# The last block's row sums, the first accumulation and the first scores of the second head pair, moved in a fused attention kernel

## The chip, the cores and the metric

The kernel runs on one core of a Trainium2 chip. The metric is the device time of one execution in microseconds (us); a version's time is the median of its runs. TensorE does matrix products (PE in the profile, its weight loads PEld), VectorE (DVE) and GpSimd (POOL) elementwise work, ScalarE (ACT) functions, copies and scalings, and SyncE (SP) issues most transfers. Each engine works through its own list of instructions in order; semaphores make one wait for another.

## What is computed

Two layers, one after the other, on x of 4 batches x 64 x 64 x 256 (float32):

```python
# layer 0: self-attention over the 4096 positions of a batch
f = xt @ Wf + bf; g = xt @ Wg + bg; v = xt @ Wh + bh
beta = softmax(einsum('bqd,bkd->bqk', g, f), axis=-1)
x = x + (einsum('bqk,bkd->bqd', beta, v) @ Wo + bo)
# layer 1: triangular attention, 8 heads of 32, then a perceptron
q, k, v1, v2 = (x @ W).reshape(B, N, N, 8, 32)  # for Wq, Wk, Wv1, Wv2
att = softmax(einsum('bilhd,bljhd->biljh', q, k) / sqrt(32), axis=2)
out = einsum('biljh,bilhd,bljhd->bijhd', att, v1, v2)
h = layer_norm(x + out @ Wo)
out = layer_norm(relu(h @ W1 + b1) @ W2 + b2 + h)
```

## The kernel before

The batches are worked through one after the other; what is left of a batch (output projection, norms and perceptron of layer 1) is spread over layer 1 of the next batch. The order of every instruction is written out by hand; there is no scheduler behind it.

**Layer 0** takes the 4096 query positions in 8 blocks of 512. For each block, 32 tiles of scores s (128 keys x 512 queries, line 534) go through an exponential on ScalarE (e, line 546) into the value product o on TensorE (line 561). VectorE adds the exponentials up in esum, four tiles side by side (line 568). At the end of a block, line 571 folds four partial sums into two, and lines 573 to 575 make of these two a pair of tiles: `part[0]` is the sum rounded to float32r (a format that TensorE takes in one pass), `part[1]` the remainder; between them line 574 writes the full sum into esum as well. In `norm`, line 582, two matmuls with a matrix of ones add both over the partitions into den; VectorE takes the reciprocal (line 584) and multiplies o by it (line 586). The projection y follows (lines 607, 608), and then q, k, v1, v2 of layer 1. Seven of the eight blocks do this behind the next block's scores. The last one has no next block: its chain esum, den, reciprocal, oT, y stands at the exit of the layer. There the matmuls hp ("heads", lines 1043 and 1048, the output projection of layer 1 of the batch before) and the rest of the projections of block 6 are put between. The full sum and den also go into a table of bounds (line 594). At the very end of the kernel that table decides whether everything is run once more in a safe form; it isn't, for these data.

**Layer 1** takes the 8 heads in 4 pairs of 2, and each pair in 8 steps: 32 steps. A step's weights come from S (exponentials of the scores sp, lines 872 and 882) through sums, es and a transposition att (line 926). Eight products of the step, m = 0 to 7, multiply att by v2 (line 974): m of 5 and more, in an even step of batches 1 to 3, on GpSimd (Rp), the others on VectorE (R). TensorE adds each up with v1 in two PSUM tiles acc (line 984; a pair of m for each n = m // 2), which ScalarE copies out as ao (line 994). The tile att is copied for GpSimd by ScalarE (attP, line 934), because GpSimd reads it there.

In batches 1 to 3 the order of all this is the list `ORDER` (line 43), walked once per period of two steps in `next_layer1` (line 1508). A word names a piece of work, and the number behind the slash how many periods late it is: `R05/1` is product m = 5 of step 0 of the period before, `A05/1` its accumulation, `T01/1` the copy ao of acc tile 1. `sp` (scores), `e0` and `e1` (their exponentials) stand at one place for all periods but the first; in the first, `sf`, `f0` and `f1` take their place later on. `h1` and `h0` are the two halves of the heads of the tile of 256 tokens two ahead, and the transfer of the next A tile is issued when both halves are made; `ht` the transposition htp of h; `hU` and `hT` its norms on ScalarE (line 1148); `m0` the first half of the perceptron (mp, line 1176), `z0` and `z1` the second (zp, line 1196). `so`, `rr`, `pp`, `fo`, `fa` are the statistics, roots, polish (GpSimd, lines 1104 to 1115) and scalings (ScalarE, line 1120) of the norms: `fo` writes z from zp, `fa` writes h from hp. All words that are not in reach of the first periods do nothing there. So the first period in which accumulations run has, on TensorE, the order A05, A04, z0, z1, t1, A03, A06, A02, A00, A07, A01, t0, sf, h1, h0, ht, A13, A12, A17.

Buffers that matter: PSUM tiles are taken from three pools of two buffers each: `psA` (1024 wide: s, sp, acc and the last block's den), `psB` (512 wide: hp, zp, mp, htp, projections), `psC` (o, att). The SBUF tile `part` shares its buffer with the perceptron's hid and the input tile xin. A transfer takes one of eight semaphores in turn, and is issued only when that semaphore's last transfer has landed; SP and ScalarE each issue from their own list.

## Time and profile before

| | us |
|---|---|
| median of 3 runs | 3689.03 |
| lowest, highest | 3687.88, 3690.12 |
| the profiled execution | 3685.46 |
| its span, from the first to the last instruction | 3683.3 |

The profiled execution is a run of its own; 2.16 us of its time lie outside the span. The mean granted clock of TensorE over the span is 0.994 of full speed. The exits of layer 0 lie at these times: the reciprocal of the last block starts at 411.40 in batch 0, 1276.33 in batch 1, some 2157.3 in batch 2 (its second den matmul starts at 2156.78) and 3038.36 in batch 3. The first scores of the second head pair, sp, start in batches 1 to 3 at 1330.46, 2211.47 and 3092.47.

Times within the span count from its start. A line of the timeline merges neighbouring instructions of one kind: start, time from the first's start to the last's end, engine, line, operation, output<-inputs, shapes, number; in brackets the idle time of the engine before it and what ended it. An fp32 matmul shows as two instructions, its two passes.

### The profile page before, as it was taken

How to read it: one execution, taken by the hardware profiler on the slowest of the kernel's cores; microseconds unless marked ns; L12 is line 12 of the kernel's file. 1: busy time of each engine (PE TensorE's matmuls, PEld its weight loads, DVE VectorE, ACT ScalarE, POOL GpSimd, SP SyncE). 2: the span in 40 equal slices, each digit the busy share in tenths (PEclk: the TensorE clock that was granted, in tenths of full speed). 3: DMA queues.
4: the chain of work that ended last, by engine and by line, in shares of the span. 5: the costliest groups of instructions: out<-in, count | busy, mean ns of one | idle time of the engine just before them, and what ended most of it. 6: DMA issues, size and time to landing. Idle time of an engine off the chain costs nothing.

```text
span 3683.3 us, 58564 instructions
## 1 busy us (share of the span) xinstructions
PE 3562.0 (97%) x22602; PEld 1930.0 (52%) x22602; DVE 2682.3 (73%) x2142; ACT 1963.3 (53%) x4257; POOL 1763.0 (48%) x918
## 2 busy tenths in 40 slices
PE   9999999988999999999999999999899999999998
PEld 6555444444555555554455555554355555555477
DVE  4555599896555569999555449999755456999976
ACT  3444456554444367665444447676544436677654
POOL 5000199895000079999100019999700005999920
PEclk9999999999999999999999999999999999999999
DMA  9111566566111344425311154333511125431221
GB/s 150 47 46 46 145 160 165 147 160 161 49 52 52 94 117 95 93 50 103 70 54 52 49 142 92 75 91 65 118 43 49 52 74 137 97 91 49 68 65 56
DMA packets 461872, 324.01 MB, mean 88 GB/s; under 512 B 300112, under 2 KB 418640, under 8 KB 452752
## 3 DMA queue, kind: packets, MB, share of 16 engines
q1 hardware_dynamic: 412544, 293.21, 29.9%
q0 software_dynamic: 36160, 19.94, 4.6%
q10 hardware_dynamic: 12880, 7.01, 0.7%
q8 instruction: 181, 2.97, 0.4%
q14 instruction: 107, 0.88, 0.1%
HBM read 176.37 MB, written 143.65 MB: 87 GB/s over the span
## 4 chain that ended last, share of the span: by engine, by line
PE 70%; POOL 7%; issue 3%; DMA 3%; DVE 3%; ACT 2%; SPq 0%; ACTq 0%; POOLq 0%; DVEq 0%
PE acc L984 18%; PE o L561 18%; POOL Rp L974 6%; PE proj L622 6%; PE zp L1196 5%; PE mp L1176 5%; PE s L534 5%; PE hp L1043 3%; PE sp L872 3%; PE v1p L654 2%; DVE R L974 1%; PE y L607 1%; PE att L926 1%; PE hp L1048 1%; PE htp L1143 1%
## 5 line engine op out<-in xcount | busy, mean ns | idle before, releaser
L974 POOL TENSOR_TENSOR Rp<-attP,v 128x2048 f32<-128x2048 f32 x328 | 1491.8, 4576 | 420.0 <-ACT attP L934 370.2
L974 DVE TENSOR_TENSOR R<-att,v 128x2048 f32<-128x2048 f32 x696 | 1548.9, 2274 | 91.0 <-PE acc L984 72.5
L561 PE MATMUL o<-e,v 128*128 128x512 f32 x2048 | 1043.4, 592 | 0.0
L568 DVE TENSOR_TENSOR esum<-esum,e 128x2048 f32<-128x2048 f32 x224 | 512.9, 2290 | 551.7 <-ACT e L546 548.8
L546 ACT ACTIVATE e<-s 128x1024 f32<-128x1024 f32 x512 | 524.0, 1025 | 581.5 <-PE s L534 481.9
L534 PE MATMUL s<-gT,fT 128*128 128x512 f32 x1024 | 785.5, 769 | 8.9 <-ACT e L546 5.1
L984 PE MATMUL acc<-R,wsel 128*32 128x512 f32 x5568 | 698.2, 599 | 16.1 <-DVE R L974 8.1
L1104 POOL TENSOR_SCALAR nt<-mv 128x4 f32<-128x4 f32 (+1 forms) x51 | 9.9, 194 | 1202.9 <-DVE mv L1060 1198.8
L561 PEld LDWEIGHTS o<-e,v 128*128 128x128 f32 x2048 | 388.3, 190 | 276.6 <-issue 233.9
L984 PE MATMUL acc<-Rp,wsel 128*32 128x512 f32 x2624 | 346.6, 600 | 27.2 <-POOL Rp L974 26.5
L994 ACT COPY ao<-acc 128x1024 f32<-128x1024 f32 x256 | 254.8, 1021 | 177.3 <-PE acc L984 166.7
L984 PEld LDWEIGHTS acc<-R,wsel 128*32 128x32 f32 x5568 | 154.7, 109 | 354.5 <-issue 277.3
L534 PEld LDWEIGHTS s<-gT,fT 128*128 128x128 f32 x1024 | 193.9, 190 | 244.4 <-issue 231.4
L909 ACT ACTIVATE es<-S,rd 128x64 f32<-128x64 f32 x1024 | 257.8, 336 | 16.2 <-DVE rd L901 13.4
L1176 PE MATMUL mp<-hT,w 128*128 128x256 f32 x1024 | 249.5, 389 | 0.7 <-ACT hT L1148 0.7
L1196 PE MATMUL zp<-w,hid 128*128 128x256 f32 x1024 | 244.9, 384 | 0.8 <-ACT hid L1185 0.8
L1176 PEld LDWEIGHTS mp<-hT,w 128*128 128x128 f32 x1024 | 186.5, 190 | 101.4 <-ACT hid L1185 36.9
L1196 PEld LDWEIGHTS zp<-w,hid 128*128 128x128 f32 x1024 | 185.5, 190 | 62.5 <-issue 31.9
L584 DVE RECIPROCAL rec<-den 128x512 f32<-128x512 f32 x32 | 107.4, 3357 | 133.6 <-PE den L582 133.6
L984 PEld LDWEIGHTS acc<-Rp,wsel 128*32 128x32 f32 x2624 | 80.2, 110 | 209.1 <-issue 124.8
L1185 ACT ACTIVATE hid<-mp,b_sb 128x256 f32<-128x256 f32 x256 | 105.6, 471 | 117.5 <-PE mp L1176 117.5
L882 ACT ACTIVATE S<-sp 128x512 f32<-128x512 f32 x128 | 129.8, 1116 | 62.9 <-PE sp L872 62.9
(179 smaller groups left out, 3595.1 us busy)
## 6 DMA issues: line engine op xcount, KB each, us to landing
v<-v2d SPq DMA_DIRECT2D x44, 512.0 KB
v1c<-v1d SPq DMA_DIRECT2D x128, 128.0 KB
aT<-ao SPq DMA_DIRECT2D x1024, 16.0 KB
A<-aT SPq DMA_DIRECT2D x256, 64.0 KB
out_dram<-z SPq DMA_DIRECT2D x63, 256.0 KB
y<-yT SPq DMA_DIRECT2D x56, 256.0 KB
q<-st SPq DMA_DIRECT2D x56, 256.0 KB
k<-st SPq DMA_DIRECT2D x52, 256.0 KB
```

The source lines that it names most:

```text
L534: nc.tensor.matmul(s_ps[r // 2][:, r % 2, :], fT[tt][:, ts(r * 4 + n, P)], gT[qb // 4][:, ts(qb % 4, QB)], start=True, stop=not safe,)
L546: nc.scalar.activation(e[g][:, 2 * j : 2 * j + 2, :], s_ps[j], AF.Exp)
L561: nc.tensor.matmul(o_ps[qb], F.v[tt][:, r * 4 + n, :], es[:, r, :], start=(k == 0 and r == 0), stop=(k == 7 and r == 3),)
L568: nc.vector.tensor_tensor(esum[qb], esum[qb], es, ALU.add)
L622: nc.tensor.matmul(ps, w[:, cc, rows], y(qb, cc), start=(cc == 0), stop=(cc == 1))
L882: nc.scalar.activation(self.S[pair][:, :, l0 : l0 + 8].rearrange("p i l -> p l i"), sp[:, lh], AF.Copy if self.safe else AF.Exp,)
L909: nc.scalar.mul(e[:, i, :], rows[:, i, :], rec[:, i : i + 1])
L974: eng.tensor_tensor(R, src.unsqueeze(1).to_broadcast([P, D, N]), v2[h], ALU.mult)
L984: nc.tensor.matmul(acc[32 * c : 32 * c + 32, n % 2, :], w[:, n, c, 16 * h : 16 * h + 32], R[:, ts(c, 8), :].rearrange("p d j -> p (d j)"), ...
L994: nc.scalar.copy(self.ao[step][:, ts(np, 2)].rearrange("p k d j -> p k (d j)"), self.acc[step][np])
L1176: nc.tensor.matmul(self.mp[:, fc % 2, :], w1_sb[:, cc, ts(fc, P)], self.hT[tt][:, cc, :], start=(cc == 0), stop=(cc == 1),)
L1196: nc.tensor.matmul(zp[:, n, :], self.hid[tt][:, fc, ts(n, P)], w2_sb[:, fc, :], start=(fc == 0), stop=(fc == 3 and tt not in self.hT2),)
```

## The change

Three edits. The last block of layer 0 (each batch) no longer makes the pair `part`: it writes only the full sum, and one fp32 matmul with the ones read as fp32 takes it to den. In the first period of a batch's layer 1 (batches 1 to 3) the accumulation A05 (of GpSimd's product) is taken out of its place and put behind A04 (of VectorE's product). And `sf`, the first scores of the second pair, moves in `ORDER` from before `R17` and `h1` to behind `h1`; `h0` moves from behind `f0` to before it. In all other periods `sf` and `f0` do nothing, so there the order stays what it was.

```diff
@@ ORDER
-    rr/1 pp/1 W0 R01/1 A07/1 A01/1 fo/1 fa T01/1 R12/1 t0 T00/1 sf/1 R17/1 h1/-1 R13/1 f0/1 h0/-1 ht f1/1 R16/1
+    rr/1 pp/1 W0 R01/1 A07/1 A01/1 fo/1 fa T01/1 R12/1 t0 T00/1 R17/1 h1/-1 sf/1 R13/1 h0/-1 f0/1 ht f1/1 R16/1
@@ values
                 nc.vector.tensor_tensor(halves[:, 0:2], halves[:, 0:2], halves[:, 2:4], ALU.add)
+                if qb == last:
+                    nc.vector.tensor_tensor(halves[:, 2], halves[:, 0], halves[:, 1], ALU.add)
+                    return
                 part = parts_of[qb] = work.tile([P, 2, QB], PART, tag="hid", name="part", bufs=1)
@@ norm
-            two = parts_of.pop(qb)
-            for h in range(2):
-                nc.tensor.matmul(den, ones_f, two[:, h], start=(h == 0), stop=(h == 1))
+            if qb < last:
+                two = parts_of.pop(qb)
+                for h in range(2):
+                    nc.tensor.matmul(den, ones_f, two[:, h], start=(h == 0), stop=(h == 1))
+            else:
+                nc.tensor.matmul(den, ones_f.bitcast(F32), part, start=True, stop=True)
@@ next_layer1
                 i = period - late
-                if word[0] in "RATSWVtc":
+                if i == 0 and word in ("A05", "A04"):
+                    for m in (4, 5) if word == "A04" else ():
+                        step_word("A", 0, m)
+                elif word[0] in "RATSWVtc":
                     step_word(word[0], 2 * i + int(word[1]), int(word[-1]))
```

## The prediction

> **What bounds the kernel now.** I read the page first: the engines' shares, then the chain of waits.

> ```profile
> span 3683.3 us, 58564 instructions
> PE 3562.0 (97%) x22602; PEld 1930.0 (52%) x22602; DVE 2682.3 (73%) x2142; ACT 1963.3 (53%) x4257; POOL 1763.0 (48%) x918
> PE 70%; POOL 7%; issue 3%; DMA 3%; DVE 3%; ACT 2%; SPq 0%; ACTq 0%; POOLq 0%; DVEq 0%
> ```

> TensorE is busy 97% of the span and carries 70% of the chain. So a saving counts only where TensorE stands still, and the edits lie at such places: the exit of the attention layer (four batches) and the first steps of the second layer (batches 1 to 3, counted from 0). I then read the timeline at the exit of batch 1, VectorE first:

> ```profile
> 1272.45 1.23 DVE L571 TENSOR_TENSOR esum<-esum 128x1024 f32<-128x1024 f32 x1
> 1273.71 0.69 DVE L573 TENSOR_TENSOR part<-esum 128x512 fp32r<-128x512 f32 x1
> 1274.32 0.69 DVE L574 TENSOR_TENSOR esum<-esum 128x512 f32<-128x512 f32 x1
> 1275.04 0.69 DVE L575 TENSOR_TENSOR part<-esum,part 128x512 fp32r<-128x512 f32 x1
> 1276.33 3.36 DVE L584 RECIPROCAL rec<-den 128x512 f32<-128x512 f32 x1 [0.59 <-PE den L582]
> ```

> Columns: start, duration, engine, line, instruction, and in brackets the idle time before it and who ended it. TensorE's waits between 1273 and 1340 us:

> ```profile
> PE sp L872 <- ACT ao L994: 1.6, 1, 1.6
> PE acc L984 <- POOL Rp L974: 1.3, 1, 1.3
> PE den L582 <- DVE part L573: 1.2, 1, 1.2
> PE den L582 <- DVE part L575: 0.8, 1, 0.8
> ```

> These four are nearly all its idle time here, and each has an edit. Its timeline around the first two:

> ```profile
> 1316.53 1.07 PE L984 MATMUL acc<-Rp,wsel 128*32 128x512 f32 x8 [1.34 <-POOL Rp L974]
> 1317.41 1.04 PE L984 MATMUL acc<-R,wsel 128*32 128x512 f32 x8
> 1318.38 1.99 PE L1196 MATMUL zp<-w,hid 128*128 128x256 f32 x8
> ...
> 1328.20 0.65 PE L926 MATMUL att<-ident,es 128*128 128x128 f32 x4
> 1330.46 2.08 PE L872 MATMUL sp<-q,k 32*64 32x64 f32 x64 [1.61 <-ACT ao L994]
> 1332.47 1.13 PE L1043 MATMUL hp<-wo,A 128*128 128x256 f32 x4
> 1333.44 0.38 PE L1048 MATMUL hp<-ident,yc 128*128 128x128 f32 x2
> 1333.66 1.03 PE L1043 MATMUL hp<-wo,A 128*128 128x256 f32 x4
> ```

> and what ScalarE does meanwhile:

> ```profile
> 1327.57 1.02 ACT L1120 ACTIVATE z<-zp,rn 128x256 f32<-128x256 f32 x2 [0.62 <-POOL rn L1115]
> 1328.48 1.02 ACT L1120 ACTIVATE h<-hp,rn 128x256 f32<-128x256 f32 x2
> 1329.38 1.94 ACT L994 COPY ao<-acc 128x1024 f32<-128x1024 f32 x2
> ```

> Batch 2 has the same pattern 881.01 us later. Batch 3 differs in one thing; one row per stretch (length, busy time of the engines, TensorE's granted clock, DMA share, GB/s):

> ```profile
> 1328.00:1335.00 7.00, 5.39 (x87) 4.48 (x84) 4.93 (x3) 5.29 (x8) 7.00 (x2) 1.00 0.35 55
> 3090.00:3097.00 7.00, 5.41 (x80) 4.28 (x77) 4.95 (x3) 5.29 (x8) 7.00 (x2) 0.84 0.33 53
> ```

> The clock falls there: sp starts at 3092.47 and the next accumulation at 3098.96, 6.49 us; in batch 1 it is 1330.46 to 1335.27, 4.81 us. The fall costs 1.68 us, and the delay stays: two periods on, the sp at 3135.14 lies 42.67 us behind, in batch 1 (1371.45) 40.99. So time won or lost here is carried on.

> [...] the heads stand 1.61 us behind an sp that waits. [...] here the two y stores hold SP for 6.07 us (1285.60 on).

> **Part 1, the row sums.** Two VectorE additions (L573, L575, 0.69 each) and one of two single-pass matmuls go; one fp32 matmul of two passes comes. The full sum takes L573's place, 1273.71 to 1274.40, so the matmul starts where den starts now, 1274.55. A pair of fp32 passes of this shape takes 1.02 us (o<-e,v x2), so it ends at 1275.57 and the reciprocal starts 0.04 later, 1275.61 instead of 1276.33: 0.72 us. TensorE is free for the heads after 2 x 0.43 us (ten o passes in 4.45), at 1275.41 instead of 1276.13: 0.72 too. What comes next is y, which waits for the product after the reciprocal (0.29 us idle), so both sides move together. Batch 0: 409.63 + 1.02 + 0.04 = 410.69 instead of 411.40, 0.71. Four batches: 2.87 us. The v2 loads, which don't move, are no new bound: the last rows land at 1302.3 in the chain of waits, and the first product starts at 1311.9.

> **Part 2, the accumulations of the first step.** VectorE's product (A04) is done at about 1314.1 (half of its pair from 1311.88), TensorE has finished its heads at about 1315.0, so A04's 0.86 us run inside the 1.34 us of idle time. A05 starts at 1316.53 as now, when GpSimd's first product is there. zp starts at 1317.50 instead of 1318.38: 0.88 us earlier. But GpSimd multiplies without a break from 1311.93 to 1325.52 (three products in 13.59), only then polishes (1325.61), and ScalarE's z, h and ao follow that. ao does not move, so sp does not: the 0.88 us become idle time before the next piece. I count it at 0; both ends of its bound are 0 to 0.1.

> **Part 3, the scores behind the heads.** In the built program the first head's matmuls stand ahead of sp; the other half and htp behind. They need a free PSUM buffer: the semaphore value they wait for is that of z (ends 1328.59), not of h (1329.50). The A tile is no bound: it was issued from 1315.0 on, ahead of the q and k loads in the same queue, whose transfers end at 1330. So the first head runs from about 1328.65, takes 1.08 us (1332.47 to 1333.66 is 1.19 behind sp, the other half 1.08) and ends at 1329.75. sp starts at 1330.46 as before, when ao ends. Behind it only one half is left, so htp starts at 1333.66 instead of 1334.74: 1.08 us. If the buffer came only with h, sp would slip by 0.19 and 0.89 us stay. ScalarE's hT then waits for S (ends 1334.56), not for htp, and ends at about 1336.5; the mp that needs it comes at 1336.9. Tight, but it fits. GpSimd has 1.71 us of slack there. No DMA issue changes place: the load that follows the heads is still behind the ao stores on SP (1331.35 to 1336.81). Three batches: 3.24 us.

> Sum: 2.87 + 3.24 = 6.1 us.

> **The clock.** From 1328.85 to 1332.47 the kernel before gives TensorE nothing but idle time and 32x64 matmuls. After, a dense head of 1.08 us splits that stretch, and the idle time at the first accumulation halves. So I expect the fall of batch 3 to go: 1.7 us. It isn't shown anywhere what it takes to keep the clock; the bounds are 0 and, since other executions may fall in all three batches, 5.0 us.

> **The forecast and its rivals.** Against the profiled execution (3685.46, span 3683.3 and 2.16 around it) the sum gives 3685.46 - 6.1 - 1.7 = 3677.7. The median of the runs, 3689.03, is 3.57 above that execution; I apply the same 7.8 us to it.

> - Forecast (0.50): 3681.2 us, its own range 3680 to 3682.5.
> - The clock falls as often as before (0.22): only 6.1, 3682.9. For it: [...] sp still has idle time around it. Against it: the dense head between.
> - The runs of before lost clock in all three batches and no longer do (0.13): 6.1 + 5.0 = 11.1, 3677.9. For it: the 3.57 us between median and profile would be two more falls (3.4). Against it: other places fall too (415 us, 445 us).
> - The head doesn't fit in the gap, so that sp is pushed back by as much as the head takes (0.09): only part 1, 2.9, 3686.1. For it: ao, z and h all sit behind one polish. Against it: the semaphore value.
> - Slower (0.06): SP's queue. In the built program the first y store takes a DMA semaphore whose last user is ScalarE's k store (issued 1288.41) instead of a v2 load. SP waits in order, and behind it stand the v2 rows and the A tile of the next heads (last issue ends 1305.88, use 1312.86). A landing of about 2.8 us (the v2 piece in the chain) leaves 4.2 us. From a slip of 4.2 + 6.1/3 = 6.2 us per batch the change loses; a slip of 12 would give 3 x 7.8 - 6.1 = +17.3, 3706. Against it: the second y store waited for that k store already, until 1291, so the rest of the queue should stand where it stood.

> **How the numbers follow.** About 0.2% (7.4 us, below 3681.65) is what a measurement can tell from no change. The forecast lies just below it: I give three quarters of its 0.50, all of the 0.13 and a fifth of the 0.22 to faster, 0.55; the rest of these and the 0.09 to within, 0.39; slower 0.06. The range leaves out the slow case and the ends of the others: 3677 to 3686.5.

> **What would show it.** The last block's reciprocal 1.2 us after the end of the full sum (now 1.93 after L573's), with one den wait instead of two; acc<-R before acc<-Rp with an idle time of about 0.5 us; a head of 1.1 us between att and sp; sp waiting for ao by 0.6 to 0.7 us instead of 1.6; htp 1.1 us closer to sp; clock 1.00 behind sp in batch 3. I am wrong if sp starts later against ao than 0.1 us, if heads wait for A, or if the clock falls in more places.

## The result, and the profile after

| | before | after |
|---|---|---|
| median of 8 runs, us | 3688.9 | 3677.18 |
| lowest, highest | 3686.57, 3692.3 | 3672.98, 3681.57 |
| the profiled execution | 3685.46 | 3672.98 |
| its span, granted clock | 3683.3, 0.994 | 3671.1, 0.995 |

The ratio of the times is 0.9968, with a 95% interval of 0.9957 to 0.9979: 11.8 us less, 7.7 to 15.9. The forecast was 3681.2 with a range of 3677.0 to 3686.5, so the time lies at the lower end of the range. The changed kernel was run once more among the experiments: 3677.01 us, ratio 0.9970 (0.9958 to 0.9982).

The page of the changed kernel: span, engines, chain of waits.

```profile
span 3671.1 us, 58563 instructions
PE 3562.7 (97%) x22602; PEld 1928.7 (53%) x22602; DVE 2676.8 (73%) x2134; ACT 1962.8 (53%) x4257; POOL 1761.7 (48%) x918
PE 79%; POOL 8%; issue 4%; DVE 4%; DMA 2%; ACT 2%; SPq 0%; ACTq 0%; POOLq 0%; DVEq 0%
```

TensorE is busy as long as before (3562.7 against 3562.0 us); by the page, the 12.2 us that the span is shorter are idle time of TensorE. A fall of the clock is here a stretch in which the traces record half of the clock as granted (0.50 of full speed from 3096 to 3098 us in the kernel before). In one of them the same matmuls had longer records (1.63 us instead of 1.13, shown below), so a fall should add busy time. Outside the last 12 us of the kernel the clock stood at half for 11 windows of 3.41 us before and for 9 after, so two windows less in these two executions, and an estimate of what one costs is at most half of its 3.41 us, 1.7. The total of the busy time doesn't show this; the profile models the ends of the matmuls in it. TensorE's waits between 1266 and 1333 us, the stretch of batch 1 that corresponds to the one shown for before:

```profile
PE den L588 <- DVE esum L573: 1.2, 1, 1.2
PE hp L1049 <- ACT z L1126: 0.6, 1, 0.6
PE sp L878 <- ACT ao L1000: 0.5, 1, 0.5
PE proj L628 <- ACT stage L691: 0.4, 1, 0.4
PE acc L990 <- POOL Rp L980: 0.4, 1, 0.4
PE y L613 <- DVE oT L592: 0.3, 1, 0.3
```

(Lines behind the edits moved: den 582 is now 588, the product 974 is 980, sp 872 is 878, ao 994 is 1000, hp 1043 and 1048 are 1049 and 1054, htp 1143 is 1149.) One of the two den waits is gone, that for GpSimd's product is 0.4 instead of 1.3, and that of sp for ao 0.5 instead of 1.6; a new one, of hp for z, took 0.6 of it. The timeline at the exit of batch 1, TensorE and VectorE:

```profile
1266.67 1.22 DVE L571 TENSOR_TENSOR esum<-esum 128x1024 f32<-128x1024 f32 x1
1267.92 0.69 DVE L573 TENSOR_TENSOR esum<-esum 128x512 f32<-128x512 f32 x1
...
1268.76 1.10 PE L588 MATMUL den<-esum,ones_f 128*128 128x512 f32 x2 [1.23 <-DVE esum L573]
...
1269.90 3.36 DVE L590 RECIPROCAL rec<-den 128x512 f32<-128x512 f32 x1 [1.28 <-PE den L588]
```

The reciprocal starts 3.23 us behind the start of L571, before 3.88 (1276.33 - 1272.45). TensorE in the first steps of layer 1:

```profile
1308.69 1.07 PE L990 MATMUL acc<-R,wsel 128*32 128x512 f32 x8
1310.12 1.06 PE L990 MATMUL acc<-Rp,wsel 128*32 128x512 f32 x8 [0.36 <-POOL Rp L980]
1311.11 1.99 PE L1202 MATMUL zp<-w,hid 128*128 128x256 f32 x8
...
1321.01 0.66 PE L932 MATMUL att<-ident,es 128*128 128x128 f32 x4
1322.22 1.13 PE L1049 MATMUL hp<-wo,A 128*128 128x256 f32 x4 [0.55 <-ACT z L1126]
1323.19 0.38 PE L1054 MATMUL hp<-ident,yc 128*128 128x128 f32 x2
1324.04 2.08 PE L878 MATMUL sp<-q,k 32*64 32x64 f32 x64 [0.47 <-ACT ao L1000]
1326.05 1.13 PE L1049 MATMUL hp<-wo,A 128*128 128x256 f32 x4
1327.01 0.38 PE L1054 MATMUL hp<-ident,yc 128*128 128x128 f32 x2
1327.23 0.60 PE L1149 MATMUL htp<-ident,h 128*128 128x128 f32 x4
```

The head stands in the gap behind z, as forecast, and htp starts 3.19 us behind sp instead of 4.28 (1334.74 - 1330.46).

Set side by side, milestone by milestone, the two spans differ like this (us, a minus is time won):

| stretch | difference |
|---|---|
| up to the fold L571 of batch 0 (no edit acts there) | -1.34 |
| exit of batch 0: row sums -0.39, a fall of the clock less -1.55 | -1.94 |
| batch 0's layer 1, up to the fold of batch 1 (no edit acts) | -2.50 |
| exits of batches 1, 2, 3: row sums | -0.65, -0.65, -0.64 |
| scores behind the head in batches 1, 2, 3 | -1.08, -1.09, -1.08 |
| batch 3: a fall of the clock behind sp less | -1.68 |
| remaining layer 1 of batches 1, 2 and 3 | +0.67, +0.03, -0.20 |

The edits' own path makes 5.58 of the 12.2 us, falls of the clock at two places 3.23, and the rest of 3.4 lies in stretches that no edit touches. The fall at the exit of batch 0 is not the edit's gain either: two other kernels with the new row sums (the row sums alone, and the change without the accumulations) had it. The 1.34 us hold a fall at 43 us that the later execution lacks. What the 2.50 are is open, since both executions have five windows at half clock there; but in thirteen of the fourteen profiles taken here batch 0's layer 1 does the same work, and from its first GpSimd product to the next fold it took between 827.0 us (with 5.1 us of clock lost between 640 and 850 us) and 834.1 (with 8.5), so that 2.5 us is well within what executions differ by.

### The profile page after: what moved, and what is told of

It reads as the page before. It is cut to its first block, busy times and chain, and to the rows that moved or that the text cites. A ratio compares the mean times of both kernels' runs of the same rounds, so it can differ in the third digit from the quotient of the medians.

```text
span 3671.1 us, 58563 instructions
## 1 busy us (share of the span) xinstructions
PE 3562.7 (97%) x22602; PEld 1928.7 (53%) x22602; DVE 2676.8 (73%) x2134; ACT 1962.8 (53%) x4257; POOL 1761.7 (48%) x918
## 4 chain that ended last, share of the span: by engine, by line
PE 79%; POOL 8%; issue 4%; DVE 4%; DMA 2%; ACT 2%; SPq 0%; ACTq 0%; POOLq 0%; DVEq 0%
PE o L561 24%; PE acc L990 16%; PE proj L628 8%; POOL Rp L980 7%; PE s L534 6%; PE mp L1182 5%; PE zp L1202 5%; PE sp L878 3%; PE hp L1049 3%; DVE R L980 2%; PE v1p L660 2%; PE y L613 2%; PE att L932 1%; PE htp L1149 1%; PE hp L1054 1%
```

## What was to be told apart

The sum of the prediction was 6.1 us of path plus 1.7 of clock; measured were 11.8. Two theories for the rest:

- **Clock.** The edits also take away places at which the clock falls, and more of them than the one that was counted.
- **Path.** Some edit, the accumulations above all, which were counted at 0, gains more on the path than the trace of one execution shows; or the difference is only that of two lucky and unlucky sets of runs.

Below, "P0" is the start of GpSimd's first product of a batch's layer 1, counted from the fold L571 of that batch's last block; it measures the exit. "htp-sp" measures the gap around the moved scores. In every profile either had one of few values. With the old row sums P0 is 39.48 or 40.60, with the new ones 38.83; htp-sp is 4.28 in the old order, or about 5.9 (once 5.39), and 3.20 with the scores behind the head. The larger value of each pair always goes with a granted clock below 1.00 in that stretch: over the 16 us behind the fold 0.89, over the 20 to 21 us from the start of zp on 0.91 or 0.92. The ratios compare with runs of the kernel before on the same chips; its median was 3687.36 us beside the first four experiments, then 3688.5, then 3689.49. A gain in us is taken from the ratio; it can differ from the difference of the two medians (for the scores alone 3.3 and 5.7).

## Experiments: each edit alone

**Row sums alone.** The hunks at `values` and `norm`, on the kernel before:

```diff
+                if qb == last:
+                    nc.vector.tensor_tensor(halves[:, 2], halves[:, 0], halves[:, 1], ALU.add)
+                    return
...
+                nc.tensor.matmul(den, ones_f.bitcast(F32), part, start=True, stop=True)
```

> Only the last block's row sums are changed (in all four batches). Path theory: den pair 0.64 us earlier in batches 1 to 3 and 0.4 in batch 0, so 2.3 us in all, a median of about 3686.6 beside 3688.9. Rival, the first exit: what the changed kernel has gained beyond the path (11.7 less 5.6) comes from batch 0, where this edit alone acts; then this run gains 6 us or more, below 3683.

Measured 3682.01 us against 3687.36, ratio 0.9989 (0.9981 to 0.9997): 4.1 us less (1.1 to 7.0). The 2.3 us of the path and the 6 us of the first exit both lie in this interval, so the time alone doesn't choose between them. P0 is 38.83 in all three batches, and at the first exit the reciprocal comes 0.39 us earlier, as in the whole change.

**Scores alone.** Only the line of `ORDER`:

```diff
-    ... t0 T00/1 sf/1 R17/1 h1/-1 R13/1 f0/1 h0/-1 ht ...
+    ... t0 T00/1 R17/1 h1/-1 sf/1 R13/1 h0/-1 f0/1 ht ...
```

> Only the scores of the second pair are put behind the first half of the heads (batches 1 to 3). Path theory: 1.08 us for each of three batches, 3.2 us, a median of about 3685.7; the two other idle times in front stay 1.34 and 0.7 us. Rival, the clock: the idle stretch before sp let the clock fall in most batches of the kernel before (1.7 us each), and a dense head in it ends that; then 5 to 8 us, 3681 to 3684.

Measured 3681.63 against 3687.36, ratio 0.9991 (0.9983 to 0.9999): 3.3 us less (0.4 to 6.3). htp-sp is 3.20 in all three batches. But P0 is 40.60, 40.60 and 40.58: the clock fell at all three exits of this profile.

**Accumulations alone.** Only the hunk of `next_layer1`:

```diff
+                if i == 0 and word in ("A05", "A04"):
+                    for m in (4, 5) if word == "A04" else ():
+                        step_word("A", 0, m)
```

> Only the first step's accumulation of VectorE's product is put first (batches 1 to 3). Path theory: zp comes 0.86 us earlier, the polish on GpSimd and so ao and sp don't move, gain 0, a median of 3688 to 3690. Rival: the 0.86 us are kept, 2.6 us. Second rival, the clock: the idle time before sp grows from 1.6 to 2.5 us, so the clock falls more often there and it is slower by up to 3 us.

Measured 3690.31 against 3687.36, ratio 1.0012 (1.0004 to 1.0019): 4.4 us slower (1.5 to 7.0). The edit is not without effect: zp starts 5.61 us behind the first product instead of 6.45, and the time that it wins is idle again before sp, which grows from 1.6 to 2.4. TensorE in batch 1 of this kernel:

```profile
1326.78 0.66 PE L926 MATMUL att<-ident,es 128*128 128x128 f32 x4
1329.80 2.08 PE L872 MATMUL sp<-q,k 32*64 32x64 f32 x64 [2.36 <-ACT ao L994]
1331.81 1.63 PE L1043 MATMUL hp<-wo,A 128*128 128x256 f32 x4
1333.24 0.63 PE L1048 MATMUL hp<-ident,yc 128*128 128x128 f32 x2
1333.66 1.91 PE L1043 MATMUL hp<-wo,A 128*128 128x256 f32 x4
```

The heads took 1.63, 0.63 and 1.91 us instead of the 1.13, 0.38 and 1.03 that stand in the changed kernel's and in the former timeline: the same instructions at half the clock.

## Experiments: the change without one of its parts

**Without the row sums.** The changed kernel with the two old additions and the two den matmuls:

```diff
-                if qb == last:
-                    nc.vector.tensor_tensor(halves[:, 2], halves[:, 0], halves[:, 1], ALU.add)
-                    return
...
+            two = parts_of.pop(qb)
+            for h in range(2):
+                nc.tensor.matmul(den, ones_f, two[:, h], start=(h == 0), stop=(h == 1))
```

> The changed kernel with the old row sums in the last block: both changes of order alone. Path theory: 3.2 us, a median of about 3685.7, as the scores alone. Rival of the first exit: also only 3.2, since batch 0 is as before; the clock rival: 5 to 8 us, 3681 to 3684.

Measured 3683.97 against 3687.36, ratio 0.9994 (0.9986 to 1.0002). htp-sp is 3.20 throughout, and P0 40.61, 40.59 and 40.59. TensorE at the exit of batch 1, and below it 7 us of that exit in one row (length, busy time of TensorE, its weight loads, VectorE, ScalarE and GpSimd with the numbers of instructions, granted clock, DMA share, GB/s):

```profile
1278.87 0.47 PE L582 MATMUL den<-part,ones_f 128*128 128x512 f32 x1 [1.23 <-DVE part L573]
1280.11 0.51 PE L582 MATMUL den<-part,ones_f 128*128 128x512 f32 x1 [0.77 <-DVE part L575]
1280.45 1.62 PE L1043 MATMUL hp<-wo,A 128*128 128x256 f32 x4
1281.87 0.63 PE L1048 MATMUL hp<-ident,yc 128*128 128x128 f32 x2
1282.29 1.91 PE L1043 MATMUL hp<-wo,A 128*128 128x256 f32 x4
```

```profile
1279.00:1286.00 7.00, 6.23 (x18) 4.05 (x19) 5.07 (x4) 0.00 (x0) 0.00 (x0) 0.76 1.00 223
```

and the corresponding stretch of the changed kernel:

```profile
1268.89:1275.89 7.00, 6.71 (x22) 3.44 (x22) 4.74 (x3) 0.59 (x1) 0.00 (x0) 1.00 0.98 214
```

With the old row sums TensorE has two idle stretches, 1.23 and 0.77 us, with 0.47 us of work between them, and in the next 3.4 us the heads run at half speed. The reciprocal doesn't wait for the heads (it starts 3.87 us behind L571, as in the kernel before; only where a fall begins ahead of den's end is it later, up to 4.06), but the heads and the projection behind them now outlast it, y comes later, and P0 is 1.12 us behind.

**Without the accumulations.** The changed kernel with the hunk of `next_layer1` taken back:

```diff
-                if i == 0 and word in ("A05", "A04"):
-                    for m in (4, 5) if word == "A04" else ():
-                        step_word("A", 0, m)
```

> The changed kernel with the old order of the first two accumulations: row sums and scores alone. Path theory: that edit is worth nothing on the path, so this equals the changed kernel, about 3677 if its other gains are of the two edits that are left in. Rival: the edit halves an idle time of TensorE and so keeps the clock; then 2 to 4 us slower than the changed kernel.

Measured 3679.21 against 3688.5, ratio 0.9976 (0.9966 to 0.9985). The first accumulation behind htp stands 22.23 us behind the first product; in the changed kernel it is 22.26 to 22.28, in the kernel before 23.34. So on this path the edit is worth nothing, as forecast, and the scores 1.08. The interval overlaps with that of the whole change. The median is 2.2 us above that of the changed kernel run beside it, within the 2 to 4 us that the rival named, so the times alone don't exclude the rival.

**The change once more,** beside these:

> The changed kernel once more, as the yardstick for the others: a median of 3677 within 2 us. If it lies above 3680, part of the 11.7 us was chance.

Measured 3677.01 against 3688.5, ratio 0.9970 (0.9958 to 0.9982).

## Experiments: the clock by itself

That idle time makes the clock fall was the author's assumption up to here. If it holds, work that nobody uses must keep the clock. The extra matmul takes an fp32 tile of 128x512 into a PSUM tile that nothing reads:

```python
def dense(n):
    ps = pb("dense")
    for _ in range(n):
        nc.tensor.matmul(ps, ident, w1_sb[:, 0, :], start=True, stop=True)
```

**In the gap before sp.** The kernel before, batches 1 to 3:

```diff
                     if (i == 0) == (word == "sf"):
+                        if i == 0:
+                            dense(1)
                         scores(i)
```

> The kernel before, with one more fp32 matmul of 128x512 (0.86 us, its result is not used) in front of the second pair's first scores in batches 1 to 3, where TensorE waits for ao anyway. Path theory alone: no gain, 3688.9. Clock theory: the stretch is no longer without dense work, the clock falls less often there: 1 to 5 us, and the profile shows a clock of 1.00 behind sp in all three batches.

Measured 3685.87 against 3688.5, ratio 0.9993 (0.9985 to 1.0001). htp-sp is 4.28 in all three: no fall behind sp, but one profile of three batches says little, and the interval includes 1.

**At the exit of batch 0.** The kernel before, two of them in 2.55 us of idle time:

```diff
         proj(last - 1, "k", 1, None, stage[0][:, 0, :])
+        if late:
+            dense(2)
         output(last)
```

> The kernel before, with two more fp32 matmuls of 128x512 (1.7 us, results not used) in batch 0 between the projection k and y, where TensorE waits 2.55 us for the reciprocal and the product. Path theory alone: no gain. Clock theory: the fall at 415 us (y at half speed, 1.5 us) goes, up to 1.5 us; rival of the first exit: what follows in batch 0 shifts as well and gains more, 3 us or more.

Measured 3687.7 against 3688.5, ratio 1.0003 (0.9995 to 1.0012). There is no fall at the exit of batch 0 (P0 33.84; with a fall, 35.1 to 35.5 in the kernels with the old row sums). Two kernels without this filler had none there in their profiles either (33.84 too). But the kernel doesn't gain: in this profile the clock fell at two later exits and once behind sp.

**At the exits of batches 1 to 3.** The kernel before; the unused matmul goes into the unused half of den's own PSUM tile, ahead of den:

```diff
-            den, part = pb("den") if qb < last else pa("den")[:, 0, :], esum.pop(qb)[:, 2, :]
+            full = None if qb < last else pa("den")
+            den, part = pb("den") if qb < last else full[:, 0, :], esum.pop(qb)[:, 2, :]
+            if qb == last and not late:
+                nc.tensor.matmul(full[:, 1, :], ident, w1_sb[:, 0, :], start=True, stop=True)
```

> The kernel before, with one fp32 matmul of 128x512 (0.86 us on TensorE, its result is used by nothing) ahead of the last block's first den matmul in batches 1 to 3, where TensorE otherwise stands idle for 1.23 us. It removes nothing. Theory (the row-sum edit gains twice: 0.65 us of path per exit, and by taking idle time from TensorE there it keeps the clock, which with the old row sums fell at 10 of 18 exits of batches 1 to 3 seen so far and cost 1.12 us each time): with the idle time filled the clock doesn't fall at any of the three exits (granted clock 1.00 in the 16 us from the fold of the sums on, first GpSimd product 39.5 us behind it and not 40.6), the reciprocal stays 3.87 us behind the fold, and the median is some 1.9 us below before, about 3686.5. Rival (what keeps the clock there is not the idle time but the later matmuls, or chance): falls at one or two of the three exits as in the other kernels with the old row sums, median as before, 3688.5. If the reciprocal comes later than 3.9 us the matmul is in the way and the run says little.

Measured 3685.67 against 3689.49, ratio 0.9990 (0.9982 to 0.9999): 3.7 us less (0.4 to 6.6), by work that only was added. TensorE at the exit of batch 1:

```profile
1275.94 1.02 PE L582 MATMUL den<-w,ident 128*128 128x512 f32 x2
1277.24 0.50 PE L585 MATMUL den<-part,ones_f 128*128 128x512 f32 x1 [0.28 <-DVE part L573]
1278.57 0.50 PE L585 MATMUL den<-part,ones_f 128*128 128x512 f32 x1 [0.82 <-DVE part L575]
1278.91 1.02 PE L1046 MATMUL hp<-wo,A 128*128 128x256 f32 x4
1279.77 0.38 PE L1051 MATMUL hp<-ident,yc 128*128 128x128 f32 x2
1279.99 1.03 PE L1046 MATMUL hp<-wo,A 128*128 128x256 f32 x4
```

The reciprocal is where it was (3.88 behind L571), the heads run at full speed, and P0 is 39.48, 39.48 and 39.47.

**In the gap that the accumulations lengthen.** The accumulation edit alone, with two unused matmuls before sp:

```diff
                     if (i == 0) == (word == "sf"):
+                        if i == 0:
+                            dense(2)
                         scores(i)
```

> The accumulation edit alone, which ran some 3 us slower than the kernel before (3690.3), plus two fp32 matmuls of 128x512 whose result is used by nothing (1.7 us) in TensorE's idle time before the first scores of the second head pair in batches 1 to 3, which that edit had lengthened from 1.6 to 2.5 us. Theory A (the edit is slow by itself because the longer idle time lets the clock fall more often there, 1.68 us each): the falls behind sp are gone in all three batches, heads stand 3.2 us + 1.1 behind sp, and the median comes down to that of the same filler on the kernel before, about 3686 to 3686.5. Theory B (it is slow for a reason elsewhere, for example transfers or the phase of later falls): the median stays at 3689 to 3691.

Measured 3688.67 against 3689.49, ratio 0.9998 (0.9990 to 1.0007). htp-sp is 4.18 in all three batches, no fall behind sp; sp starts 1.18 us behind the start of ao's copy instead of 1.08, so the two matmuls are in its way by 0.1. The slowdown of the accumulations alone is gone, but the intervals touch (1.0004 to 1.0019 without), and the one profile without the filler showed a fall behind sp in one batch of three only. That the longer idle time is why it is slow fits; that it is all of the 4.4 us isn't settled.

**Two tries for more.** The changed kernel with the filled exit of batch 0, and the same with three more unused matmuls in the idle time of batch 0's first step, where every other profile has at least two windows at half clock (6.83 us from 442.6 us on in the kernel before):

```diff
             e = self.e.pop(step)
+            if self.b == 0 and step < 2:
+                dense(1)
...
                 elif word[0] in "RATSWVtc":
+                    if i == 0 and word == "A05":
+                        dense(1)
```

> The changed kernel plus two fp32 matmuls of 128x512 whose result is used by nothing, at the exit of batch 0, in 2.5 us of idle time before y. Theory (the clock falls at the exit of batch 0 in some executions of every kernel, 1.6 us each; the changed kernel's own profiles showed none): none there, the first GpSimd product of batch 0 is 33.5 us behind the fold, and the median is 0 to 1 us below the changed kernel's, 3676 to 3677. Rival: what follows in batch 0's layer 1 shifts its falls, so that nothing is kept: 3677 to 3679.

> As the run with the filled exit of batch 0, and one more such matmul (0.86 us) in each of three more idle stretches of batch 0's first step of layer 1 (1.7, 1.4 and 1.7 us, before the first two transpositions and before the first accumulation), where every profile so far shows two falls of the clock, 3.4 us of clock between 438 and 450 us. Theory (a fall needs idle time, and each costs about what it loses): one or both falls go, 1.7 to 3.4 us, median 3673 to 3675.5. Rival (the stretch waits for ScalarE and GpSimd, not for TensorE, so that the falls there cost little, or the filler delays the transpositions): the falls go or stay, and the median stays at 3676 to 3678.

Measured 3679.15 (ratio 0.9974, 0.9964 to 0.9983) and 3678.23 (0.9973, 0.9963 to 0.9984) against 3689.49. The exit of batch 0 has no fall (P0 33.45 in both), but the changed kernel's own two profiles had none there either. In the second kernel one of the two windows at half clock between 440 and 450 us is gone. Neither ratio is below the changed kernel's. No version here beats it.

## The falls counted

All fourteen profiles together, in batches 1 to 3:

| place | kernels | falls | cost of one |
|---|---|---|---|
| exit, old row sums | before and six experiments | 11 of 21 | 1.12 us |
| exit, new row sums | after and five experiments | 0 of 18 | |
| exit, old row sums, filled | one experiment | 0 of 3 | |
| behind sp, old order | before and four experiments | 4 of 15 | 1.63 to 1.68 us (once 1.11) |
| behind sp, scores behind the head | after and six experiments | 0 of 21 | |
| behind sp, old order, filled | two experiments | 0 of 6 | |

The exits of one execution are not independent (all three fell in two kernels, none in two others), so the safer count is of profiles: with the old row sums 5 of 7 show a fall at an exit, with the new ones 0 of 6. Drawing 5 such among 13 at random would put all into the seven with a chance of 21/1287, 2%. Behind sp it is 4 of 5 profiles against 0 of 9, 5/1001, 0.5%.

```profile
1277.34:1280.75 3.41, 1.41 (x5) 0.75 (x5) 2.74 (x5) 0.00 (x0) 0.00 (x0) 1.00 1.07 244
1280.75:1284.16 3.41, 3.41 (x11) 2.54 (x10) 3.38 (x2) 0.00 (x0) 0.00 (x0) 0.50 0.95 212
```

```profile
1272.09:1275.50 3.41, 1.70 (x4) 0.38 (x2) 3.31 (x5) 0.00 (x0) 0.00 (x0) 1.00 1.00 234
1275.50:1278.91 3.41, 3.12 (x15) 2.53 (x16) 2.82 (x2) 0.00 (x0) 0.00 (x0) 1.00 1.02 224
```

```profile
1266.49:1269.90 3.41, 2.19 (x6) 0.87 (x5) 2.06 (x4) 0.00 (x0) 0.00 (x0) 1.00 1.04 242
1269.90:1273.31 3.41, 3.41 (x16) 2.25 (x14) 3.38 (x2) 0.00 (x0) 0.00 (x0) 1.00 1.02 226
```

At the 21 exits with the old row sums this leaves no exception. In the 11 with a fall one window holds both idle stretches whole, and TensorE is busy in it for 1.41 or 1.42 us. In the 10 others the border of two windows cuts through the exit, and the emptier one holds 1.70 us or more. With the new row sums no position of a window at the exits of batches 1 to 3 holds less than 2.18 us, with the filled exit 2.31. In all profiles together, from the start of the clock record on, a window at full clock was followed by a fall in all 98 cases with under 1.4 us of busy time, in 41 of 63 from 1.4 to 1.6, in 15 of 444 from 1.6 to 2.6, and in none of some 14250 above that. All of the 15 hold transpositions or sp.

Behind sp the busy time alone doesn't sort the cases. It does if the 32x64 matmuls of sp are counted at half of their time: then the windows ahead of the four falls hold at most 1.55 us, and all others there 1.58 or more. (The half is an estimate, fitted to these cases; shares from 0.3 on sort them too, with a lower border.) Counted so, the worst position of a window holds 0.9 us in the old order, 0.5 with the accumulations alone, and at least 1.7 with the scores behind the head or a filled gap. So by these counts both edits take away the emptiest windows, and were not only lucky: among the positions of the raster, those that went with a fall no longer occur there. A batch takes 881.0 us, which is 258.1 windows, so from batch to batch the raster moves by only 0.37 us against the work. That fits the exits of one execution going together.

By these counts the old row sums cost on average 11/21 x 3 x 1.12 = 1.8 us of falls, and the old order 4/15 x 3 x 1.68 = 1.3 us. Both rest on few profiles, and on some of the same kernels as the ratios below. With the path (0.39 + 0.65 + 0.65 + 0.65 = 2.3 for the row sums, 3 x 1.08 = 3.2 for the scores) that makes sums to compare with the ratios:

| kernel | sum | measured (interval) |
|---|---|---|
| the change | -8.7 | -11.8 (-15.9 to -7.7), again -11.1 (-15.5 to -6.6) |
| row sums alone | -4.1 | -4.1 (-7.0 to -1.1) |
| scores alone | -4.6 | -3.3 (-6.3 to -0.4) |
| accumulations alone | 0 | +4.4 (+1.5 to +7.0) |
| without row sums | -4.6 | -2.2 (-5.2 to +0.7) |
| without accumulations | -8.7 | -8.9 (-12.5 to -5.5) |
| filled before sp | -1.3 | -2.6 (-5.5 to +0.4) |
| filled exits of 1 to 3 | -1.8 | -3.7 (-6.6 to -0.4) |

In all but the accumulations alone the interval holds the sum. For these accumulations, the share of raster positions that lead to a fall behind sp rises from 0.6 to 0.9 by the count above; that makes 0.3 x 3 x 1.68 = 1.5 us more, an estimate at the lower end of the interval. Left out are the filled exit of batch 0 on the kernel before (+1.1, -1.8 to +4.4), the filler behind the accumulations (-0.7, -3.7 to +2.6) and the two tries on the changed kernel (-9.6 and -10.0), whose sums need the falls of batch 0. The whole change measured 2.4 to 3.1 us more than its sum, within its interval; whether that is chance or a further gain of the three edits together stays open.

## Why the prediction was right, and where its terms were off

**Direction and mechanism** held. The three edits act where the prediction put them, and the steps it named to be checked read so: one den wait instead of two; the reciprocal 1.29 us behind the end of the full sum; acc<-R first, with 0.36 us of idle time before acc<-Rp (about 0.5 said); a head between att and sp; sp waiting by 0.5 instead of 1.6 (0.6 to 0.7 said); htp 1.08 us closer; clock 1.00 in the stretch of batch 3:

```profile
3082.20:3089.20 7.00, 6.54 (x100) 4.20 (x101) 3.75 (x3) 5.74 (x11) 7.00 (x2) 1.00 0.13 23
```

**Part 1, 2.87 us, became 2.34.** In batches 1 to 3 it won 0.65, not 0.72: the pair of fp32 passes of den took 1.10 us, not the 1.02 of the o matmuls it was taken from (a float32r matmul of the old den is one instruction, 0.47 and 0.50 us in batch 1). In batch 0 it won 0.39, not 0.71. The prediction started the new den at 409.63, where the old one's record starts; that record was 0.72 us long, against 0.47 in batch 1, and lay over the o matmuls before it. TensorE still worked at these, as the two timelines show, before and after:

```profile
406.52 3.60 PE L561 MATMUL o<-e,v 128*128 128x512 f32 x8
409.63 0.72 PE L582 MATMUL den<-part,ones_f 128*128 128x512 f32 x1
410.86 0.50 PE L582 MATMUL den<-part,ones_f 128*128 128x512 f32 x1 [0.52 <-DVE part L575]
```

```profile
405.18 3.60 PE L561 MATMUL o<-e,v 128*128 128x512 f32 x8
408.61 1.02 PE L588 MATMUL den<-esum,ones_f 128*128 128x512 f32 x2
```

Behind the start of o, den starts 3.43 us after instead of 3.11, with no idle time. In batch 0 the matmuls, not the sum, were last.

**Part 2, 0 us,** held on the path: ao starts 17.4 to 17.5 us behind the first product with the edit and without it. What wasn't foreseen is that the edit alone makes the kernel slower. In the change the head takes the idle time that the edit lengthens, and there no harm was measured.

**Part 3, 3.24 us,** came out as 1.08, 1.09 and 1.08. The buffer came free with z, and hT, which ended at 1329.83 (1327.93 + 1.90), was in time for its mp at 1330.47.

**The clock, 1.7 us,** is the term that was mis-sized. That idle time and 32x64 matmuls let the clock fall was the author's estimate; the trace of before showed a fall behind them in one batch of three (half clock for 3.41 us from 3094.8 on) and not what it takes. The runs fit it: with the head in the gap the emptiest position of a window holds at least 1.7 us instead of 0.9 (sp at half), and the fall of batch 3 went. But the step "So I expect the fall of batch 3 to go: 1.7 us" took falls to exist where one profile showed one, behind sp, and applied that to the median. By the counts the median holds 1.3 us there and 1.8 at the exits, where the profile of before happened to show none in batches 1 to 3. The second is a gain of the row sums that the prediction hadn't named anywhere, though the two den waits that it showed are the idle time in question. Nor was it mere chance which batch fell: in all fourteen profiles the fall goes with where the windows lie.

All terms corrected, the sum is 8.7 us instead of the 7.8 of the forecast. That explains 0.9 of the 4.0 us by which the time lies below 3681.2; the other 3.1 stay open, within the interval of 7.7 to 15.9. It is in part luck that the time lies in the stated range: it is 0.2 us from the lower end, and the range reached so far down for a rival whose cause did not hold.

**The rivals.** The one whose number fits best (3677.9, falls behind sp in all three batches) doesn't fit in its cause: the old order fell there in 4 cases of 15, and in no profile in more than one batch. Falls as often as before, and a head that doesn't fit, are excluded by the tables above. The slower one, SP's queue, did not come. SP does wait within its list: in the kernel before, the two y stores held it for 6.07 us, 5.3 of them until ScalarE's k store had landed, and its next transfer came at 1291.76. The second y store was issued later against L571 (its issue ended 20.89 us behind it, before 19.22), as that rival had it, but the A tile's last issue ended 30.82 us behind L571 instead of 33.43, and no head waited for it.

## What to carry to other kernels

In this kernel a short idle stretch of TensorE cost twice: its own length (1.23 and 0.77 us at an exit), and a fall of the clock behind it that came in some executions only (11 of 21 exits, 1.12 us each). So read the raster of the falls from the traces (3.413 us in these), look at how much work one of its windows can hold at worst around such a stretch, and count the falls over several profiles, before pricing an edit that fills or opens it. Moving work that is needed anyway into the gap was the best filler here, since it wins on the path too (1.08 us a time plus the falls). A saving that only lengthened the idle time before the next fixed point was not free (the accumulations alone, 4.4 us slower).

## What was not expected of the hardware

The clock fell behind short idle stretches of TensorE: behind 1.23 and 0.77 us with 0.47 us of matmul between, in 11 of 21 cases, and behind 1.6 us (with the accumulations alone 2.4) followed by 2 us of 32x64 matmuls, in 4 of 15. Little tipped it: 1.23 us alone gave no fall in 18 cases, and with one unused matmul of 1.02 us in the first of the two stretches there was none in 3. What sorts the exits in these traces is not the length of one gap but the sum in a window of the raster: 1.41 or 1.42 us of busy time in 3.41, about 2 us idle in all, went with a fall in 11 cases, and 1.70 or more with none in 10. In all profiles together, under 1.4 us was followed by a fall in all 98 cases.

A fall lasted one or more windows of 3.413 us, and one of a single window cost 1.12 us at the exits, where the reciprocal of 3.36 us runs beside the heads, and mostly 1.63 to 1.68 behind sp. By busy time alone the windows behind sp don't sort; with the 32x64 matmuls of sp counted at about half, the estimate above, they do (at most 1.55 us ahead of the four falls, 1.58 or more elsewhere). How the transpositions count, which stand in most of the other exceptions, was not worked out.
